# First queries in pieces, batch 1's keys first, base 3 summed with bases 0 to 2, and batch 1's copies on other queues

## The chip, the core and the metric

The kernel runs on one core of a Trainium2 chip. A core has five engines with an instruction queue each: TensorE (PE, matrix products into PSUM), VectorE (DVE), ScalarE (ACT), GpSimd (POOL) and SyncE (SP, which here only issues DMAs). ACT and POOL can issue DMAs too, in their own queues. An engine takes its queue in order, so an instruction that waits holds up everything behind it on that engine. The metric is the device time of one execution in microseconds (us), as the median of several runs.

## What is computed

Eight sequences of 256 tokens of width 512 pass through a gated attention block and a gated feed forward:

```python
x = x + tanh(g_xattn) * attention(layernorm(x), ctx)      # 32 heads of 16, 8 key heads
x = x + tanh(g_ffn) * feed_forward(layernorm(x))

# attention
q = heads(concat([ctx, h]) @ Wq)                          # Wq 1024 x 512
k, v = heads(h @ Wk), heads(h @ Wv)
ssm_k, ssm_v = heads(ctx @ Wsk), heads(ctx @ Wsv)
scores = q @ [ssm_k, k].T / sqrt(16) + alibi              # each query sees 64 keys back, in both halves
o = softmax(scores) @ [ssm_v, v];  return o @ Wo

# feed forward
probs = softmax(xt @ w_router);  topk of 4 among 128 experts
gate, up = xt @ w_gate, xt @ w_up                         # 8 bases of 256 columns
basis = silu(gate) * up
mixed = weighted sum of the 8 bases, weights from the experts' squared amplitudes
return mixed @ w_down + silu(xt @ sg) * (xt @ su) @ sd    # sg, su: two more pieces of 256 columns
```

## The kernel before

**Batches and stages.** A batch is one sequence: two tiles of 128 tokens. For each of the eight batches there are four stages: `project` (norm, transposes, keys, queries, values), `attention`, two `tail`s (one for each tile: output projection, second norm, transposes, router) and `feed_forward`. They are generators that issue a few instructions and yield a weight; `run` takes the one with the smallest time first, so that the work of one batch's attention and the next but one batch's projection is laid between the products of a batch's feed forward. `start(gen, length, at, total)` sets the pace of a generator. The order on every engine's queue is fixed in this way when the program is built; on the chip nothing is reordered.

**The start.** Loads stand first (lines 112 to 145): the context `ctT` of batch 0 and the first half of its `x` on SP; `wsk`, the first half of `wq`, `wk`, the second half of `x`, the second half of `wq`, `wsv`, `wv` and batch 1's `x` and context on ACT, ahead of ACT's table load (`warm`). PE runs 14 transposes of the identity (`idle`, line 171). `project_first` then makes the first tile's keys (`pk`, line 389) and queries (`pq`, line 402), group by group in four banks, and transposes `x`. `rest` makes batch 0's values and the second tile's keys and queries between the steps of its attention, and goes on with `project(1)`. The bank that it takes alternates between the tag `one` and `gu2`.

**Attention.** `score` makes the products of queries and keys (line 628), `soften` adds the bias and takes the smallest value (DVE, line 641), `exponentials` runs on ACT (660), `divide` on POOL (672), `turn` transposes blocks on DVE (685), `values` multiplies by the values (PE, 707). The values lie in `vbd`, copied by DMA from `vpad` (`diagonals`, line 496) in 16 copies for each batch: SP and POOL issue them for batch 0, SP alone for the others. `first_batch` is batch 0's form.

**Feed forward.** There are ten pieces `k` of 256 columns: eight bases, two shared pieces. Each is a product of two by two blocks, done as seven block products (Winograd's form) instead of eight; it needs sums of weight blocks. The tokens' sums `sT` are made for each batch, the weights' sums once: `sub` subtracts two blocks (line 953), `keep` stores the result in device memory (957), and later batches load it (`load_gu`: 7 loads of 256 KB for a summed piece, 4 for one that isn't). A piece's loads are issued two pieces ahead, when the block that used the buffer is done (`after`). For bases 2, 0 and 1, in this order, `first_weights` sums during batch 0's attention, all on POOL; for pieces 3 to 9 the first feed forward does it, in the piece ahead (`more`, `late`), the first two subtractions on DVE and the other two on POOL. `wgu` holds two pieces at a time.

The block products of a piece go to two PSUM banks: `m15` and then `m76`, then 2 and 3 into the first, 4 into the second. ACT copies `u`, `m5` and `m7` out and computes the tanh `th`; a bank is free when the values in it have been used. There are three such banks.

**Steps of the tail.** `po` (line 866) is the output projection, `tr_f` the transposes of the second norm's result, `pl` the router's product, `pst` and `pc` turn the selection into coefficients, with ACT's copy `selT` between the two.

The names in the profile leave numbers out: `sc<-kT,qT` is a score product, `sc<-pt,vbd` a values product, `m<-w,hT` and `m<-w,sT` block products.

Of the kernel before, what the change touches and what calls it, by code (L numbers as in the profile page):

```python
# [15 lines left out]
P = 128  # L16
# [16 lines left out]
MASKED = 1e32  # L33
WARM = 14


@with_exitstack
def gated_block(
# [93 lines left out]

    def load_queries(half):
        nc.scalar.dma_start(
            wq_sb[:, half * NC : (half + 1) * NC, :],
            wq[half * HID : (half + 1) * HID].rearrange("(c p) n -> p c n", p=P),
        )

    load_queries(0)
    wk_sb = weight(wk, HID, HK * D, "wk", nc.scalar)  # L140
    nc.scalar.dma_start(x_0[:, 1, :], x[0, P:, :])
    load_queries(1)
    wsv_sb = weight(wsv, HID, HK * D, "wsv", nc.scalar)
    wv_sb = weight(wv, HID, HK * D, "wv", nc.scalar)
    loaded[1] = load(1, nc.scalar), load_context(1, nc.scalar)

# [20 lines left out]
    warm = const.tile([P, 1], F32, tag="warm", name="warm")  # L167
    nc.scalar.activation(warm, neghalf[:, :1], AF.Tanh)
    idle = next_bank("idle")
    for _ in range(WARM):  # L170
        nc.tensor.transpose(idle[:, 0, :P], ident, ident)

# [96 lines left out]
    def first_weights():  # L269

        for k in (2, 0, 1):
            for g in range(1, 5):
                load_gu(k, g)
            if k == 2:
                yield 2.0
                later["wd"] = weight(w_down, I, HID, "wd", nc.sync)


                later["sd"] = sd = const.tile([P, NSI // 2, HID], F32, tag="sd", name="sd")
                nc.sync.dma_start(  # L280
                    sd, sw_down.rearrange("(j o p) n -> o p j n", o=2, p=P)[1]
                )
            if k == 0:
                yield 5.5
                yield from first_sums(2)
        yield 1.0
        yield from first_sums(0)
        yield 1.0
        yield from first_sums(1)
# [84 lines left out]
    def project_first():  # L374
# [25 lines left out]
        def queries(pq, g, cols, cs):  # L400
            for c in cs:
# [4 lines left out]
                )  # L406

        def put_queries(pq, g, t):
            blocks = slice(t * NB // NT, (t + 1) * NB // NT)
# [8 lines left out]
        keys(pk, 0, slice(0, T))  # L418
        evict = transposed(xnT, first_normed[0], 0, "x0", lambda shape, name: early(name, NC))
        pqs = [next_bank(f"pq_0_{g}")[:, 0, :P] for g in range(G - 1)]  # L420
        pqs.append(ps_one.tile([P, P], F32, tag="one", name="pq_0_3"))
        for g in range(G):
            queries(pqs[g], g, tiles[0], range(NC))
        put_keys(pk, 0, slice(0, T))
        evict()
        evict = transposed(xnT, first_normed[1], 1, "x0", lambda shape, name: early(name, NC))
        keys(pk, 1, tiles[0])
        for g in range(G):
            queries(pqs[g], g, tiles[0], range(NC, 2 * NC))
        put_keys(pk, 1, tiles[0])  # L430
# [76 lines left out]
    def project(b, xns=None):  # L507
# [18 lines left out]
        xnT = two.tile([P, NC, T], F32, tag="xo", name=f"xnT_{b}")  # L526
        if b == 1:
            yield BEFORE
        for t in range(NT):
            yield from own()  # L530
            evict = transposed(xnT, xns[t], t, f"x{b}", bank)
            yield AFTER if b == 1 else AFTER - 0.8
            evict()
            free()
            yield BEFORE if b == 1 else BEFORE + 0.8


        kT = two.tile([P, 2, 2, T], F32, tag="kT", name=f"kT_{b}")
        yield from own()
        pk = bank([P, 2, T], f"pk_{b}")  # L540
        for s, (w_sb, src) in enumerate(((wsk_sb, ctT), (wk_sb, xnT))):
            for c in range(NC):
# [3 lines left out]
                )  # L546
            yield AFTER if s else MORE
        for par in range(2):
# [4 lines left out]
        free()  # L553
        yield BEFORE


# [22 lines left out]
        for t in range(NT):  # L579
            for s, (w_sb, src) in enumerate(((wsv_sb, ctT), (wv_sb, xnT))):  # L580
                for c in range(NC):
# [10 lines left out]
    def attention(b):  # L592
# [185 lines left out]
        for u in range(2 * n + 4):  # L778
# [193 lines left out]
    def feed_forward(b):  # L972
# [324 lines left out]
```

## Time and profile before

| | us |
|---|---|
| median of 3 runs | 1021.93 |
| lowest and highest | 1018.09, 1021.96 |
| the profiled execution, its own time | 1023.29 |
| span of its trace | 1021.4 |
| DVE waits for the chain of PE's last output projection of batch 0 (L866) | 8.41 |
| POOL busy from 60 to 80 us, from 80 to 100 us | 14.86, 5.61 |
| PE busy from 100 to 150 us | 43.23 |
| PE busy from 150 to 200 us | 50.00 |

In the profile's windows every row is a stretch of time from the span's start, with the busy time of each engine in it; PE's granted clock is 1.00 at full speed. In the timeline a row gives the start, the duration, the engine and line, the operation, its output and inputs, the count, and in brackets how long the engine had been idle before it and who released it. `ACTq`, `SPq` and `POOL ... DMA_DIRECT2D` rows are issues of DMAs. An fp32 matrix product shows as two records.

### The profile page before, as it was taken

How to read it: one execution, taken by the hardware profiler on the slowest of the kernel's cores; microseconds unless marked ns; L12 is line 12 of the kernel's file. 1: busy time of each engine (PE TensorE's matmuls, PEld its weight loads, DVE VectorE, ACT ScalarE, POOL GpSimd, SP SyncE). 2: the span in 40 equal slices, each digit the busy share in tenths (PEclk: the TensorE clock that was granted, in tenths of full speed). 3: DMA queues.
4: the chain of work that ended last, by engine and by line, in shares of the span. 5: the costliest groups of instructions: out<-in, count | busy, mean ns of one | idle time of the engine just before them, and what ended most of it. 6: DMA issues, size and time to landing. Idle time of an engine off the chain costs nothing.

```text
span 1021.4 us, 27843 instructions
## 1 busy us (share of the span) xinstructions
PE 989.7 (97%) x10470; PEld 799.9 (78%) x10470; DVE 601.0 (59%) x2241; ACT 442.0 (43%) x1657; POOL 470.2 (46%) x892
## 2 busy tenths in 40 slices
PE   8888799899999999999999999999999999999998
PEld 8666687777888687886778868788787977787886
DVE  2764766757564675636855378544665466765453
ACT  3652454335542455415543255433554335442231
POOL 4773576734553255523644236342455225661341
PEclk9999999999999999999999999999999999999999
DMA  6942845569545694447844577455964468665891
GB/s 206 231 145 79 252 146 151 170 199 288 175 137 154 180 301 142 152 141 217 282 141 146 163 214 256 125 166 165 267 204 140 133 191 257 203 195 174 271 302 66
DMA packets 117302, 192.15 MB, mean 188 GB/s; under 512 B 12848, under 2 KB 34864, under 8 KB 117168
## 3 DMA queue, kind: packets, MB, share of 16 engines
q1 hardware_dynamic: 112672, 184.87, 58.9%
q10 hardware_dynamic: 4112, 4.46, 1.3%
q8 instruction: 83, 1.36, 0.5%
q0 software_dynamic: 384, 1.05, 0.5%
q14 instruction: 51, 0.42, 0.1%
HBM read 158.87 MB, written 14.68 MB: 170 GB/s over the span
## 4 chain that ended last, share of the span: by engine, by line
PE 87%; DVE 5%; issue 2%; POOL 2%; ACT 2%; DMA 1%; SPq 0%; ACTq 0%; DVEq 0%; POOLq 0%
PE m L1001 38%; PE m L1010 10%; PE pq L562 8%; PE sc L707 6%; PE po L866 5%; PE sc L628 5%; PE pd L1144 4%; PE pk L543 2%; PE pv L582 2%; PE pd L1147 2%; POOL pr L672 1%; PE pq L402 1%; PE pl L896 1%; DVE pr L641 1%; ACT pr L660 1%
## 5 line engine op out<-in xcount | busy, mean ns | idle before, releaser
L672 POOL TENSOR_SCALAR pr<-pr,rd 128x192 f32<-128x192 f32 (+2 forms) x512 | 210.9, 430 | 251.6 <-DVE rd L669 234.3
L660 ACT ACTIVATE pr<-pr,nm 128x192 f32<-128x192 f32 (+2 forms) x512 | 218.9, 430 | 110.0 <-DVE nm L641 58.7
L1001 PE MATMUL m<-w,sT 128*128 128x256 f32 x1024 | 253.1, 381 | 1.1 <-DMA w<-in_L_ffn_w_up 0.7
L1001 PEld LDWEIGHTS m<-w,sT 128*128 128x128 f32 x1024 | 194.5, 191 | 29.0 <-issue 1.2
L641 DVE CUSTOM_DVE_ANT_1 pr<-sc,nbias 128x192 f32<-128x192 f32 (+2 forms) x512 | 154.0, 322 | 99.8 <-PE sc L628 92.9
L1001 PE MATMUL m<-w,hT 128*128 128x256 f32 x768 | 204.9, 390 | 1.0 <-DVE u L1046 1.0
L1001 PEld LDWEIGHTS m<-w,hT 128*128 128x128 f32 x768 | 140.1, 191 | 25.6 <-issue 6.3
L1091 POOL TENSOR_TENSOR mixed<-mixed,th 128x256 f32<-128x256 f32 x112 | 81.2, 725 | 137.8 <-DVE th L1086 137.8
L685 DVE STREAM_TRANSPOSE pt<-pr 128x768 f32<-128x768 f32 (+2 forms) x128 | 111.5, 871 | 4.6 <-POOL pr L672 3.0
L660 ACT ACTIVATION_READ_ACCUMULATOR pr<-pr,nm 128x1 f32 x512 | 97.9, 191 | 0.0
L1047 POOL TENSOR_TENSOR m<-m,u 128x256 f32<-128x256 f32 x80 | 61.2, 765 | 67.8 <-DVE u L1046 58.9
L963 ACT ACTIVATE th<-m 128x256 f32<-128x256 f32 x80 | 30.8, 384 | 138.2 <-DVE up L1057 138.1
L707 PEld LDWEIGHTS sc<-pt,vbd 64*32 64x32 f32 x5120 | 61.1, 106 | 26.3 <-issue 14.2
L707 PE MATMUL sc<-pt,vbd 64*32 64x64 f32 (+2 forms) x5120 | 69.0, 229 | 9.1 <-DVE nm L641 5.2
L1069 DVE TENSOR_TENSOR gate<-u,m 128x256 f32<-128x256 f32 x80 | 33.3, 416 | 72.4 <-PE m L1001 66.9
L1057 DVE TENSOR_TENSOR up<-u,m 128x256 f32<-128x256 f32 x80 | 33.3, 417 | 67.6 <-PE m L1001 40.7
L628 PE MATMUL sc<-kT,qT 32*128 32x192 f32 (+2 forms) x1024 | 64.9, 336 | 4.6 <-DVE nm L641 4.1
L628 PEld LDWEIGHTS sc<-kT,qT 32*128 32x128 f32 x1024 | 45.1, 184 | 28.3 <-DVE nm L641 9.4
L963 ACT ACTIVATE th<-gate 128x256 f32<-128x256 f32 x80 | 33.2, 416 | 76.7 <-DVE gate L1069 76.7
L1010 PE MATMUL m<-sT,w 128*128 128x128 f32 x512 | 66.1, 278 | 0.0
L1010 PEld LDWEIGHTS m<-sT,w 128*128 128x128 f32 x512 | 62.3, 194 | 0.4
L1144 PE MATMUL pd<-sd,shT 128*128 128x512 f32 x128 | 61.5, 603 | 0.2 <-DVE shT L1080 0.2
(131 smaller groups left out, 1375.7 us busy)
## 6 DMA issues: line engine op xcount, KB each, us to landing
w<-s SPq DMA_DIRECT2D x284, 256.0 KB, 3.5
w<-in_L_ffn_w_gate SPq DMA_DIRECT2D x130, 256.0 KB, 3.1
w<-in_L_ffn_w_up SPq DMA_DIRECT2D x73, 256.0 KB, 4.0
vbd<-vpad SPq DMA_DIRECT2D x120, 128.0 KB, 3.2
s<-w SPq DMA_DIRECT2D x40, 256.0 KB, 3.4
w<-in_L_ffn_shared_w_gate SPq DMA_DIRECT2D x32, 256.0 KB, 2.7
w<-in_L_ffn_shared_w_up SPq DMA_DIRECT2D x18, 256.0 KB, 3.7
sd<-in_L_ffn_shared_w_down SPq DMA_DIRECT2D x16, 256.0 KB, 3.4
```

The costliest lines, as they stand in the source:

```text
L562: nc.tensor.matmul(pq, lhsT=wq_sb[:, c, g * P : (g + 1) * P], rhs=(ctT if c < NC else xnT)[:, c % NC, :], start=(c == 0), stop=(c == 2 * N ...
L628: nc.tensor.matmul(seen(scs[p][:, j * COLS : (j + 1) * COLS], qb), lhsT=qT[rows, qb].rearrange("p g q -> p (g q)"), rhs=kT[rows, par, :, f ...
L641: nc.vector.tensor_tensor_reduce(out=part, in0=seen(scs[p][:, j * COLS : (j + 1) * COLS], qb0 + j), in1=bass.AP(tensor=bias.tensor, offset ...
L660: nc.scalar.activation(part, part, AF.Exp, bias=nmax, scale=-1.0, accum_out=den)
L672: nc.gpsimd.tensor_scalar(part, part, rden[:, p : p + 1], 1.0, op0=ALU.mult, op1=ALU.mult)
L685: nc.vector.transpose(pt[:, u % 4].rearrange("p c (s k) -> p (c s) k", s=2)[:, :, lo:], pr.rearrange("p c (s k) -> p (c s) k", s=2)[:, :, ...
L707: nc.tensor.matmul(scs[gp][32 * c : 32 * (c + 1), 2 * COLS + lo * Q : 2 * COLS + hi * Q], lhsT=vbd[rows, kb % (P // Q), kb // (P // Q) * 2 ...
L963: nc.scalar.activation(th, gate, AF.Tanh, scale=0.5)
L1001: nc.tensor.matmul(dst, lhsT=sides_of[m][c], rhs=w[:, c, :], start=(first and c == 0), stop=(c == NC // 2 - 1), skip_group_check=True,)
L1010: nc.tensor.matmul(dst[:, cols], lhsT=w[:, c, cols], rhs=sides_of[m][c], start=(first and ic == c == 0), stop=(c == NC // 2 - 1), skip_gro ...
L1091: nc.gpsimd.tensor_add(mixed[t], mixed[t], th)
L1144: nc.tensor.matmul(po, lhsT=shT[:, ic, t * P : (t + 1) * P], rhs=down[ic], **flags)
```

## The change

First, the queries' weights come in eight loads of 256 KB instead of two of 1 MB. ACT's table load stands behind the first four; `wk`, the second half of `x` and the other four follow. `wsv`, `wv` and batch 1's input are issued by ACT only after the first eviction of `xnT`. The first tile's queries run chunk by chunk over all four groups, three chunks ahead of the transposes of `x` and one behind. The 14 transposes of the identity become 9 matrix products.

Second, in batch 1's projection the context's keys come ahead of the transposes of `x`, which use the bank `gu2`; the input's keys follow. `rest` starts its alternation with the other bank.

Third, `first_weights` sums base 3 too: the order is 2, 3, 0, 1, and its pace changes. The first feed forward sums and stores pieces 4 to 9.

Fourth, the copies to `vbd` of batch 1 are issued by ACT (two groups) and POOL (two groups) instead of SP, and batch 2's `x` and context are loaded by ACT instead of SP.

```diff
-WARM = 14
+WARM = 9
...
-    load_queries(0)
-    wk_sb = weight(wk, HID, HK * D, "wk", nc.scalar)
-    nc.scalar.dma_start(x_0[:, 1, :], x[0, P:, :])
-    load_queries(1)
-    wsv_sb = weight(wsv, HID, HK * D, "wsv", nc.scalar)
-    wv_sb = weight(wv, HID, HK * D, "wv", nc.scalar)
-    loaded[1] = load(1, nc.scalar), load_context(1, nc.scalar)
+    def load_queries(cs):
+        for c in cs:
+            nc.scalar.dma_start(wq_sb[:, c, :], wq[c * P : (c + 1) * P, :])
+
+    load_queries(range(NC))
...
     nc.scalar.activation(warm, neghalf[:, :1], AF.Tanh)
+    wk_sb = weight(wk, HID, HK * D, "wk", nc.scalar)
+    nc.scalar.dma_start(x_0[:, 1, :], x[0, P:, :])
+    load_queries(range(NC, 2 * NC))
     idle = next_bank("idle")
     for _ in range(WARM):
-        nc.tensor.transpose(idle[:, 0, :P], ident, ident)
+        nc.tensor.matmul(idle[:, 0, :P], lhsT=ident, rhs=ident, start=True, stop=True)
...
-        for k in (2, 0, 1):
+        for k in (2, 3, 0, 1):
             for g in range(1, 5):
                 load_gu(k, g)
...
-            if k == 0:
+            if k == 3:
                 yield 5.5
                 yield from first_sums(2)
+                yield 1.0
+                yield from first_sums(3)
...
+        def first_queries(pqs, cs):
+
+            for c in cs:
+                for g in range(G):
+                    queries(pqs[g], g, tiles[0], [c])
...
-        evict = transposed(xnT, first_normed[0], 0, "x0", lambda shape, name: early(name, NC))
...
-        for g in range(G):
-            queries(pqs[g], g, tiles[0], range(NC))
+        first_queries(pqs, range(NC - 1))
+        evict = transposed(xnT, first_normed[0], 0, "x0", lambda shape, name: early(name, NC))
+        first_queries(pqs, [NC - 1])
         put_keys(pk, 0, slice(0, T))
         evict()
+        wsv_sb = weight(wsv, HID, HK * D, "wsv", nc.scalar)
+        wv_sb = weight(wv, HID, HK * D, "wv", nc.scalar)
+        loaded[1] = load(1, nc.scalar), load_context(1, nc.scalar)
+        later.update(wsv=wsv_sb, wv=wv_sb)
         evict = transposed(xnT, first_normed[1], 1, "x0", lambda shape, name: early(name, NC))
         keys(pk, 1, tiles[0])
-        for g in range(G):
-            queries(pqs[g], g, tiles[0], range(NC, 2 * NC))
+        first_queries(pqs, range(NC, 2 * NC))
...
-                if banks[0] % 2:
+                if banks[0] % 2 == 0:
                     return other_bank(2, name)
...
-    def diagonals(qd, eng):
+    def diagonals(qd, *engs):
...
-            eng.dma_start(
+            engs[g * len(engs) // G].dma_start(
...
-            loaded[b] = load(b), load_context(b)
+            eng = nc.scalar if b == 2 else nc.sync
+            loaded[b] = load(b, eng), load_context(b, eng)
...
+        if b == 1:
+
+            yield BEFORE
+            yield from own()
+            pk = bank([P, 2, T], f"pk_{b}")
+            keys(pk, 0)
+            for t in range(NT):
+                yield MORE
+                evict = transposed(
+                    xnT, xns[t], t, f"x{b}",
+                    lambda shape, name: other_bank(2, name).rearrange("p (c n) -> p c n", n=P),
+                )
+                yield AFTER
+                evict()
+            yield BEFORE
+            keys(pk, 1)
+            yield AFTER
...
-                    diagonals(2 * (u - 1) + step, nc.sync)
+
+                    diagonals(2 * (u - 1) + step, *((nc.scalar, nc.gpsimd) if b == 1 else (nc.sync,)))
...
-            late = b == 0 and k > 2
-            more = b == 0 and 2 < k + 1 < PIECES
+            late = b == 0 and k > 3
+            more = b == 0 and 3 < k + 1 < PIECES
...
-    start(first_weights(), 0.39, at=-0.537, total=20.5)
+    start(first_weights(), 0.40, at=-0.537, total=25.5)
```

More of the change, by code (lines that the diff above doesn't have):

```diff
@@ L131, in gated_block @@
     wq_sb = const.tile([P, 2 * NC, HID], F32, tag="wq", name="wq")
[L133 to L137, printed above, removed]
-    load_queries(0)
-    wk_sb = weight(wk, HID, HK * D, "wk", nc.scalar)
-    nc.scalar.dma_start(x_0[:, 1, :], x[0, P:, :])
-    load_queries(1)
-    wsv_sb = weight(wsv, HID, HK * D, "wsv", nc.scalar)
-    wv_sb = weight(wv, HID, HK * D, "wv", nc.scalar)
-    loaded[1] = load(1, nc.scalar), load_context(1, nc.scalar)
+    def load_queries(cs):
+        for c in cs:
+            nc.scalar.dma_start(wq_sb[:, c, :], wq[c * P : (c + 1) * P, :])
+    load_queries(range(NC))
     ident = const.tile([P, P], F32, tag="ident", name="ident")
@@ L526, in project, with keys @@
         xnT = two.tile([P, NC, T], F32, tag="xo", name=f"xnT_{b}")
[L527 to L535, printed above, removed]
         kT = two.tile([P, 2, 2, T], F32, tag="kT", name=f"kT_{b}")
-        yield from own()
-        pk = bank([P, 2, T], f"pk_{b}")
-        for s, (w_sb, src) in enumerate(((wsk_sb, ctT), (wk_sb, xnT))):
+        def keys(pk, s):
+            w_sb, src = ((wsk_sb, ctT), (wk_sb, xnT))[s]
             for c in range(NC):
@@ L546, in project @@
                 )
-            yield AFTER if s else MORE
+        if b == 1:
[14 more added lines that the diff above has]
+            yield AFTER
+        else:
+            for t in range(NT):
+                yield from own()
+                evict = transposed(xnT, xns[t], t, f"x{b}", bank)
+                yield AFTER - 0.8
+                evict()
+                free()
+                yield BEFORE + 0.8
+            yield from own()
+            pk = bank([P, 2, T], f"pk_{b}")
+            for s in range(2):
+                keys(pk, s)
+                yield AFTER
         for par in range(2):
@@ L554, in project @@
         yield BEFORE
+        if b == 1:
+            yield BEFORE
         qT = two.tile([P, NB, G, Q], F32, tag="qT", name=f"qT_{b}")
@@ L579, in project @@
         for t in range(NT):
-            for s, (w_sb, src) in enumerate(((wsv_sb, ctT), (wv_sb, xnT))):
+            for s, (w_sb, src) in enumerate(((later["wsv"], ctT), (later["wv"], xnT))):
                 for c in range(NC):
```

## The prediction

> **What bounds the kernel now.** I read the busy shares first, then the windows by stage, then the timelines and waits of the stages that are not full. TensorE (PE) is busy 97% of the span. From 300 us on there is nothing to win: 298.64 of 300 us busy between 300 and 600. What this change touches lies before 130 us, and PE is not full there.
>
> ```profile
> PE 989.7 (97%) x10470; PEld 799.9 (78%) x10470; DVE 601.0 (59%) x2241; ACT 442.0 (43%) x1657; POOL 470.2 (46%) x892
> ```
> The windows (columns: stage and its length, busy time and instructions of PE, weight load, VectorE (DVE), ScalarE (ACT), GpSimd (POOL), then PE's granted clock, DMA share, GB/s):
>
> ```profile
> 40.00:60.00 20.00, 15.70 (x214) 11.63 (x214) 11.76 (x53) 13.20 (x54) 13.09 (x24) 0.96 0.83 251
> ...
> 95.00:100.00 5.00, 4.48 (x17) 3.89 (x18) 4.06 (x22) 2.43 (x11) 1.48 (x6) 0.66 0.58 144
> ...
> 120.00:125.00 5.00, 1.11 (x4) 0.65 (x4) 3.58 (x11) 0.48 (x2) 1.10 (x2) 0.85 0.85 315
> 125.00:130.00 5.00, 3.65 (x69) 3.13 (x70) 4.92 (x17) 2.27 (x10) 4.84 (x5) 0.50 0.02 6
> ```
> There are three soft places: the start, 42 to 97 us, and 120 to 130 us, where the clock is also halved after the idle time. As PE is full later, a microsecond won here should reach the end whole.
>
> **Part A, the start.** The timeline of PE:
>
> ```profile
> 1.37 3.25 PE L171 MATMUL idle<-ident 128*128 128x128 f32 x14 [1.37 <-POOL neghalf L150]
> ...
> 5.68 3.78 PE L389 MATMUL pk<-ctT,wsk 128*128 128x256 f32 x8 [1.07 <-DMA wsk<-in_L_xattn_Wsk]
> ...
> 10.11 4.09 PE L402 MATMUL pq<-ctT,wq 128*128 128x128 f32 x32
> ```
> Later, eight records of this keys product (L543) take 1.99 us. Here they take 3.78: PE is at half speed in spite of 14 transposes (the profile's clock column doesn't show it this early). The change makes the warm-up nine matmuls, two records each like every fp32 product here: 18 x 0.236 (half the 0.47 per 256 columns) = 4.25 us, from 1.37 to 5.6. By the row alone: full speed came with the queries, at about 10.5, 4.8 us after the first real matmul; from 1.37 that gives 6.2, and the keys end at about 7.9 instead of 9.47: 1.6 saved. The Trainium skill ("TensorE: Matmul & The Clock Gate", Parts 1 and 4) says that transposes don't count as activity, and that a free-running window of about 3.4 us must be busy. By it the clock rises between 4.8 and 8.2: 1.9 to 0.6 saved. Here the row's 1.6 stands.
>
> First queries: now all 1 MB of a half must land (1.26 + 9.0 = 10.26). In four pieces, and with wk and x's second half behind the table load, ctT, wsk, x's first half and the four pieces are 2.1 MB; the DMA rate of the first 20 us (about 1.1 MB by 5.5 us, then 380 GB/s) brings them by 8.3, so the pieces don't hold PE after the keys: three pieces 24 x 0.111 = 2.7 -> 10.6, transposes 0.44, fourth 0.9 -> 11.9. Next is late: x's second half, 2.6 MB in, lands at 9.8, its norm takes the 2.3 of now (10.63 to 12.96) -> 12.1; transposes, keys, 32 records: 0.44 + 0.89 + 3.56 -> 17.0. All four groups now end together, so four evictions of 0.29 end at 17.6, against 19.43. **A = 1.8 us** (0.6 to 2.2). wsv, wv and batch 1's input, issued at 11.3 behind the eviction, hold ACT for about 2 us (four issues of 0.5); behind them stand the second keys copy and xnT's second half, wanted only by 17; wsv lands by 14.5, wanted at 18. The table load now stands ahead of wk's issue: 1.28 us, with the pieces still in flight.
>
> **Part B, 20 to 97 us.** What goes: with batch 1's context keys first and transposes in another bank, PE's waits for ACT at 45.01 (0.70), 47.24 (1.58) and 55.18 (1.66, kT), three of four waits of 0.47 for qT, and, since po of the second half now has pq_3, pv and sc_0 behind it, 1.29 + 0.68 at 94 to 96 with their slow clock (1.5). Sum 8.8.
>
> What comes: base 3's four subtractions, 4 x 1.27 on POOL (L953; 16 instead of 12 before the first feed forward), and, as bases 2 and 3 fill the two buffers, base 0's loads only behind the last store of base 3. POOL now:
>
> ```profile
> 43.98 1.62 POOL L672 TENSOR_SCALAR pr<-pr,rd 128x192 f32<-128x192 f32 x4 [4.39 <-DVE rd L669]
> 46.22 1.62 POOL L672 TENSOR_SCALAR pr<-pr,rd 128x192 f32<-128x192 f32 x4 [0.61 <-DVE rd L669]
> 47.81 1.28 POOL L953 TENSOR_TENSOR w<-w,w 128x512 f32<-128x512 f32 x1
> ...
> 77.03 1.62 POOL L672 TENSOR_SCALAR pr<-pr,rd 128x192 f32<-128x192 f32 x4
> 78.59 0.10 POOL L905 MEMSET prob<- 128x4 f32 x1
> 78.66 2.63 POOL L953 TENSOR_TENSOR w<-w,w 128x512 f32<-128x512 f32 x2
> 92.07 0.55 POOL L184 TENSOR_TENSOR rs_f<-ve_f,neghalf 128x1 f32<-128x1 f32 x1 [10.78 <-DVE ve_f L182]
> ```
> In the changed order (times in the old clock, without A) POOL runs full from 44: last subtraction of base 3 done at 65.6, base 0's loads (SP's next in line) issued 66 to 67.7, landed 70.5; behind the first subtraction that waits for them POOL has the last two divides: subtraction, pr_14, two subtractions, pr_15: 70.5 + 1.3 + 1.6 + 2.6 + 1.6 = 77.6, against 78.65. With one transpose on DVE the last values product starts at 78.6 instead of 80.07, though PE would be there at about 73: most of the 8.8 turns into this wait. From there PE has 1.9 + 1.73 (pq_3's first half, which stood ahead of it) + po 3.43 + 1.73 + 0.67 + 1.78 + 0.76 + 0.44 + 1.78 + 0.9 = 15.1, so the feed forward starts at 93.7, not 96.8, and warm (0.9 more): 4.0. If PE cools in the 5 us wait, it loses up to 1.7 again. **B = 3.5 us** (1 to 8).
>
> **Part C, first feed forward.** PE now, by its timeline:
>
> ```profile
> 95.52 1.50 PE L896 MATMUL pl<-wr,hT 128*128 128x128 f32 x8 [0.68 <-ACT hT L205]
> ...
> 119.98 1.13 PE L1001 MATMUL m<-w,sT 128*128 128x256 f32 x4 [0.73 <-DMA w<-in_L_ffn_w_up]
> 126.35 1.55 PE L707 MATMUL sc<-pt,vbd 64*32 64x96 f32 x64 [5.24 <-DVE nm L641]
> ```
> and what DVE does meanwhile:
>
> ```profile
> 121.31 0.69 DVE L953 TENSOR_TENSOR w<-w,w 128x512 f32<-128x512 f32 x1 [3.50 <-DMA w<-in_L_ffn_w_up]
> ```
> DVE's first subtraction of base 3 waits 3.5 us for a load that SP issued at 114.78, behind the copies to vbd and batch 2's input, and that took 6.5 us to land (median 4.0). Everything on DVE behind it waits, so the values product waits 5.24. With base 3 summed before, this goes: 0.73 + 5.24 + about 2.0 at half clock = 8.0. The next candidate is base 4: its loads come one piece later, 3.5 to 5 us landing against some 6.5 us until it is wanted: no wait. Base 3's seven loads instead of four (0.75 MB more) are made good by its four stores that leave this stage.
>
> What comes: eight of sixteen vbd copies and x_2, ctT_2 stand in ACT's in-order queue, between the exponentials and PSUM copies that free PE's banks. The built program takes eight completion counters in turn for the copies of SP and ACT together, and each copy waits for the transfer that had its counter before; so the seventh vbd copy waits until x_2 has landed. On SP four such issues take 2.53 to 3.11 us, 0.65 each. Queued behind on ACT: selT (then pc on PE), th of piece 0 (then the bank of piece 1's m76), u and m5 of piece 1 (then its m23). From the feed forward's start: issues done 1.3 to 5.5, selT 6.8 (PE ready 6.3: 0.5); x_2 7.6, th 10.5, bank free 10.9 (PE ready 9.5: 1.4); x_2 landed 12.5 (+4.4 and a little, by the row of SP's x loads), two issues, four exponentials of 0.44, copies: 15.9 (PE ready 12.7: 3.2). Sum 5.1. If x_2 lands as slowly as on ACT's row at the start (8.9 us), 9.3. I take 6.5, nearer to the first, as the DMA share here (0.85 to 0.93) has SP's rows in it. POOL's eight issues of 0.57 fall into its gaps.
>
> Here a rule speaks against the change: "DMA: Bandwidth & Descriptors", Issuing engines are not separate DMA queues: all issuers share sixteen engines, spreading saves only issue time. The row agrees in what leaves SP (11.0 us of issue), but that was no wait of PE's by itself: by the rule the copies' move wins nothing and costs the 6.5; only by the row of the load stuck behind SP's copies would it have saved about 2 of the 3.5, which the early sum saves already. **C = 8.0 - 6.5 = 1.5 us** (-4 to 7).
>
> The other edits (bank parity, the values weights through a dictionary, pacing of later batches by equal numbers) change neither work nor waits.
>
> **Sum.** 1.8 + 3.5 + 1.5 = 6.8. The profiled execution took 1023.29 (span 1021.4): 1016.5 there. It is 1.4 above the median of the runs; from 1021.93 the forecast is **1015.1 us**.
>
> **Rivals.** (1) ACT's issues hide: its 43% share and its idle 1.44 us at 100.12 speak for it, the order of its queue against. 1.8 + 3.5 + 8.0 = 13.3: 1008.6. (2) Waits only move: PE cools at both new waits and x_2 lands slowly: 1.8 + 2.3 + 8.0 - 9.3 - 1.7 = 1.1: 1020.8. For it: each idle spell above was followed by a halved clock. (3) Slower: **ACT's queue** becomes the bound of the first feed forward. Its ten issues add ten times their excess over 0.65 to a chain on which PE already waits. The gain is gone when an issue costs 1.3, and at 1.9, the mean of its three slow issues at 3.66 to 9.4 (2.11, 1.71, 1.85), it is 6.8 - 12.5 = 5.7 lost: 1027.6. SP's vbd copies beside POOL's took 1.26 (10.11 for 8) with the DMA full; that this came in one burst speaks against.
>
> **Chances.** Forecast 0.42, rival 1 0.20, rival 2 0.26, rival 3 0.12. About 0.5% (5 us) is what can be told from no change: faster 0.62, same 0.26, slower 0.12. Forecast's own range 1011 to 1017; 1006 to 1023 takes in rivals 1 and 2.
>
> **What would show it.** A: keys records near 2 us and first scores at 17.6. B: an idle PE ahead of the last values product (73 to 78), released by POOL's divide; feed forward at 92. C: no DVE wait on L953's successor near 120; PE waits behind ACT's u, th, selT in the ten us after the feed forward's start. I am wrong if ACT's issues cost nothing, if base 4's subtraction waits for its loads instead, or if later batches are no longer full.

## The result, and the profile after

| | kernel before | changed kernel | ratio, 95% interval |
|---|---|---|---|
| first comparison, 6 runs each | 1019.17 | 1027.32 (1022.53 to 1031.26) | 1.0066 (1.0046 to 1.0086) |
| second comparison, 22 runs of the changed kernel | 1021.21 | 1022.85 (1018.85 to 1028.80) | 1.0019 (1.0008 to 1.0030) |
| third comparison, 22 runs of the changed kernel | 1020.89 | 1022.89 (1019.17 to 1025.93) | 1.0018 (1.0007 to 1.0028) |

The change makes the kernel slower, by 0.2 to 0.7%: the sign is the same in three comparisons, the size is not. The size goes with the granted clock: its mean over the runs was 0.985 in the first comparison, 0.990 and 0.989 in the other two; why it was lower in the first is not shown. The forecast was 1015.1, so its sign was wrong. The profiled execution of the changed kernel took 1025.07, its span 1023.3.

The page's busy times say nothing of it: PE is at 97% as before.

```profile
PE 991.4 (97%) x10474; PEld 802.0 (78%) x10474; DVE 598.8 (59%) x2239; ACT 441.4 (43%) x1657; POOL 474.5 (46%) x902
```

The windows of the changed kernel (columns as in the prediction) show where it lies:

```profile
40.00:60.00 20.00, 17.03 (x208) 12.76 (x206) 9.21 (x44) 12.00 (x50) 12.96 (x22) 0.76 0.77 239
...
95.00:100.00 5.00, 5.00 (x52) 4.75 (x51) 2.78 (x15) 2.39 (x9) 3.08 (x5) 1.00 0.28 105
...
105.00:110.00 5.00, 3.48 (x19) 2.71 (x12) 1.97 (x9) 2.08 (x10) 2.85 (x6) 0.76 1.06 285
110.00:115.00 5.00, 2.59 (x9) 1.89 (x8) 1.65 (x8) 0.38 (x1) 2.12 (x6) 0.84 1.06 300
115.00:120.00 5.00, 3.83 (x13) 2.55 (x12) 2.26 (x11) 4.10 (x17) 1.79 (x4) 0.72 1.08 304
120.00:125.00 5.00, 5.00 (x37) 4.21 (x36) 4.77 (x24) 3.73 (x17) 4.03 (x8) 1.00 1.08 268
125.00:130.00 5.00, 5.00 (x96) 4.09 (x95) 4.90 (x18) 1.75 (x9) 3.15 (x8) 1.00 0.66 223
```

The hole that stood at 120 to 130 us (PE busy 1.11 and 3.65 of 5) is gone, and one of the same kind stands at 105 to 120, with the clock below 1. From 40 to 60 us PE is busier than before because it runs at a lower clock (0.76 instead of 0.96), not because it does more.

PE's timeline, by the steps that the prediction had named:

```profile
5.89 1.99 PE L386 MATMUL pk<-ctT,wsk 128*128 128x256 f32 x8 [0.44 <-DMA wsk<-in_L_xattn_Wsk]
...
13.22 0.66 PE L199 MATMUL tr_x<-ident,xn_a 128*128 128x128 f32 x4 [1.32 <-DVE xn_a L185]
...
18.71 0.73 PE L657 MATMUL sc<-kT,qT 32*128 32x64 f32 x16 [0.37 <-ACT qT L413]
...
51.54 2.04 PE L736 MATMUL sc<-pt,vbd 64*32 64x96 f32 x112 [1.48 <-DVE pt L714]
53.51 3.40 PE L539 MATMUL pk<-xnT,wk 128*128 128x256 f32 x8
...
81.21 0.73 PE L736 MATMUL sc<-pt,vbd 64*32 64x32 f32 x48
83.60 1.67 PE L736 MATMUL sc<-pt,vbd 64*32 64x96 f32 x144 [1.67 <-DVE rrd L941]
...
98.86 1.03 PE L1031 MATMUL m<-w,hT 128*128 128x256 f32 x4
```

and in the kernel before the feed forward's first product:

```profile
96.81 1.91 PE L1001 MATMUL m<-w,hT 128*128 128x256 f32 x4
```

The warm-up works: the first keys take 1.99 instead of 3.78 us. Then PE waits 1.32 us for the second half of `x` to land and be normalized, and the first scores start at 18.71 (before 19.47, forecast 17.6). At 51.54 a values product waits 1.48 us for a transposed block, and the keys behind it take 3.40 us where eight records at full clock take 1.99. PE reaches the last values product at 81.21 and, after the first 48 of its records, waits 1.67 us, until 83.60. The feed forward starts at 98.86: before it was 96.81, the forecast was 92.

What POOL does ahead of these two waits:

```profile
46.23 2.63 POOL L983 TENSOR_TENSOR w<-w,w 128x512 f32<-128x512 f32 x2
...
75.59 1.27 POOL L983 TENSOR_TENSOR w<-w,w 128x512 f32<-128x512 f32 x1 [3.37 <-DMA w<-in_L_ffn_w_up]
```

Two subtractions in a row stand ahead of the divide (at 48.84) that PE's 51.54 needs; in the kernel before none stands there, as the divide at 46.22 follows that at 43.98 directly. And a subtraction of base 0 waits 3.37 us for its load, with the last divides behind it.

In the first feed forward ACT's timeline (`ACTq` is an issue of a DMA by ACT) and PE's list of waits (us in total, times, longest) belong together:

```profile
104.70 0.61 ACTq L502 DMA_DIRECT2D vbd<-vpad  x1
105.36 0.40 ACT L689 ACTIVATE pr<-pr,nm 128x128 f32<-128x128 f32 x1 [3.60 <-DMA w<-in_L_ffn_w_gate]
...
115.85 0.45 ACT L689 ACTIVATE pr<-pr,nm 128x192 f32<-128x192 f32 x1 [2.56 <-DMA w<-in_L_ffn_w_gate]
```

```profile
PE m L1031 <- DVE th L998: 2.4, 1, 2.4
...
PE pc L968 <- ACT selT L963: 1.5, 1, 1.5
...
PE m L1031 <- ACT m L1064: 1.2, 1, 1.2
```

The exponential at 105.36 needs no weights. What waited for the load of a gate block was the copy to `vbd` ahead of it, which stood at 101.9 to 104.7 until that load had freed its completion counter. PE's three waits are those that the prediction worked out (0.5, 1.4 and 3.2: 5.1 by its own sum; 1.5, 2.4 and 1.2 here: 5.1).

### The profile page after: what moved, and what is told of

Read it like the earlier page. It is cut to its first block, busy times and chain, and to the rows that moved or that the text cites. A ratio compares the mean times of both kernels' runs of the same rounds, so it can differ in the third digit from the quotient of the medians.

```text
span 1023.3 us, 27856 instructions
## 1 busy us (share of the span) xinstructions
PE 991.4 (97%) x10474; PEld 802.0 (78%) x10474; DVE 598.8 (59%) x2239; ACT 441.4 (43%) x1657; POOL 474.5 (46%) x902
## 4 chain that ended last, share of the span: by engine, by line
PE 84%; DVE 6%; DMA 3%; ACT 2%; POOL 2%; issue 1%; SPq 1%; ACTq 0%; DVEq 0%; POOLq 0%
PE m L1031 37%; PE m L1040 9%; PE pq L591 9%; PE sc L736 6%; PE po L896 5%; PE sc L657 5%; PE pd L1174 4%; PE pv L611 3%; PE pk L539 2%; PE pd L1177 2%; DMA w<-in_L_ffn_w_gate 1%; ACT pr L689 1%; POOL w L983 1%; POOL pr L701 1%; SPq L502 1%
## 5 line engine op out<-in xcount | busy, mean ns | idle before, releaser
L701 POOL TENSOR_SCALAR pr<-pr,rd 128x192 f32<-128x192 f32 (+2 forms) x512 | 208.8, 427 | 228.2 <-DVE rd L698 204.4
L1031 PE MATMUL m<-w,sT 128*128 128x256 f32 x1024 | 254.0, 382 | 2.4 <-DVE th L998 2.4
L736 PE MATMUL sc<-pt,vbd 64*32 64x96 f32 (+2 forms) x5120 | 71.7, 234 | 7.4 <-DVE pt L714 3.6
L657 PEld LDWEIGHTS sc<-kT,qT 32*128 32x128 f32 x1024 | 45.2, 184 | 29.1 <-DVE nm L670 10.5
```

The lines of the kernel that those rows point to most:

```text
L657: nc.tensor.matmul(seen(scs[p][:, j * COLS : (j + 1) * COLS], qb), lhsT=qT[rows, qb].rearrange("p g q -> p (g q)"), rhs=kT[rows, par, :, f ...
L701: nc.gpsimd.tensor_scalar(part, part, rden[:, p : p + 1], 1.0, op0=ALU.mult, op1=ALU.mult)
L736: nc.tensor.matmul(scs[gp][32 * c : 32 * (c + 1), 2 * COLS + lo * Q : 2 * COLS + hi * Q], lhsT=vbd[rows, kb % (P // Q), kb // (P // Q) * 2 ...
L1031: nc.tensor.matmul(dst, lhsT=sides_of[m][c], rhs=w[:, c, :], start=(first and c == 0), stop=(c == NC // 2 - 1), skip_group_check=True,)
```

## The experiments

Three marks in PE's timeline cut the path: K, the first record of batch 1's context keys; F, the first block product of batch 0's feed forward; E, the last product of the shared down projection of batch 1 (`pd<-sd`). From E to the span's end all traces take 663.5 to 665.4 us, so E stands for the end. Every kernel was compared with the kernel before on its own chip. From `start_only` on the table stands in groups of four, and the runs of one group ran on one chip. A single trace is one execution: between those of one kernel F moves by up to 3.5 us and E by up to 7, so the ratios decide on a time, and the marks on a place where several traces agree.

| run | what it has | K | F | F - K | E | E - F | ratio, 95% interval |
|---|---|---|---|---|---|---|---|
| before | | | 96.8 | | 357.2 | 260.4 | |
| changed | | 42.9 | 98.9 | 56.0 | 359.1 | 260.2 | 1.0066 (1.0046 to 1.0086) |
| start_only | start | | 96.9 | | 356.5 | 259.6 | 1.0002 (0.9990 to 1.0014) |
| start_keys | start, keys first | 40.8 | 91.5 | 50.7 | 355.4 | 263.9 | 0.9986 (0.9975 to 0.9997) |
| sp_all | changed, copies on SP | 42.3 | 97.9 | 55.5 | 361.3 | 263.4 | 1.0016 (1.0005 to 1.0027) |
| late3 | changed, base 3 late | 40.8 | 91.5 | 50.7 | 352.6 | 261.1 | 0.9963 (0.9948 to 0.9977) |
| after2 | changed | 42.6 | 99.2 | 56.5 | 361.6 | 262.4 | 1.0019 (1.0008 to 1.0030) |
| after_x2e | changed, input 2 early | 41.9 | 96.9 | 55.0 | 357.5 | 260.6 | 1.0013 (1.0001 to 1.0025) |
| late3_x2e | base 3 late, input 2 early | 42.8 | 93.6 | 50.8 | 351.9 | 258.3 | 0.9985 (0.9972 to 0.9999) |
| late3_pool_x2e | the same, copies on POOL | 42.8 | 94.7 | 51.8 | 352.5 | 257.8 | 0.9956 (0.9941 to 0.9970) |
| late3b | late3 again | 41.4 | 92.7 | 51.3 | 353.0 | 260.3 | 0.9980 (0.9968 to 0.9991) |
| late3_pool | base 3 late, copies and input 2 on POOL | 41.9 | 92.7 | 50.8 | 354.3 | 261.6 | 1.0000 (0.9987 to 1.0013) |
| after_pool | changed, copies and input 2 on POOL | 42.2 | 98.9 | 56.7 | 358.6 | 259.7 | 1.0055 (1.0035 to 1.0076) |
| pool_twice | start_keys, four more subtractions | 41.1 | 95.1 | 54.0 | 356.3 | 261.2 | 1.0015 (1.0003 to 1.0027) |
| after_c | changed | 40.9 | 96.0 | 55.2 | 356.6 | 260.6 | 1.0018 (1.0007 to 1.0028) |
| sp_all_c | sp_all again | 39.5 | 94.4 | 54.9 | 354.0 | 259.6 | 1.0006 (0.9995 to 1.0018) |
| after_pool_x2e | changed, copies on POOL, input 2 early | 42.6 | 99.3 | 56.7 | 353.3 | 254.0 | 0.9959 (0.9946 to 0.9972) |
| best_c | late3_pool_x2e again | 40.9 | 91.8 | 50.9 | 349.4 | 257.7 | 0.9937 (0.9917 to 0.9956) |

"Copies" are batch 1's sixteen to `vbd`, "input 2" is batch 2's `x` and context, 1 MB.

### The start alone

The kernel before with the diff's first part and nothing else.

> Kernel before with the start of the changed kernel alone (nine warm-up matmuls, first queries in four pieces, values weights and batch 1's input loaded later). The prediction's term for the start: 1.8 us gained whole, first scores at 17.6. What the changed kernel's trace suggests: 0.8 us gained, first scores at 18.7, PE's idle 1.3 us ahead of the second normalized half. Rival: the 0.8 us is lost again before 100 us because later loads come later (batch 1's input): no change, feed forward at 96.8 as before.

The first scores start at 18.73 (0.74 earlier), yet F is where it was, and the time is the same. PE's timeline of this run shows where the gain went:

```profile
43.70 0.66 PE L199 MATMUL tr_x<-ident,xn_a 128*128 128x128 f32 x4 [0.70 <-ACT xnT L200]
45.94 3.28 PE L548 MATMUL pk<-ctT,wsk 128*128 128x256 f32 x8 [1.58 <-ACT xnT L200]
49.15 1.28 PE L633 MATMUL sc<-kT,qT 32*128 32x192 f32 x16
```

and the same place in the kernel before:

```profile
47.24 1.99 PE L543 MATMUL pk<-ctT,wsk 128*128 128x256 f32 x8 [1.58 <-ACT xnT L205]
49.16 0.93 PE L628 MATMUL sc<-kT,qT 32*128 32x192 f32 x16
```

The new start is 1.3 us ahead there. The waits of 0.70 and 1.58 us are the same in both, but here the clock is halved behind them (0.62 and 0.53 in the windows of 46 to 50 us; 1.00 before), which costs 1.29 + 0.35 = 1.6 us. The gain is eaten at once. The rival was right that it is lost before 100 us, but not by the later loads that it named.

### Keys first, with base 3 late and all copies on SP

```diff
-        for k in (2, 3, 0, 1):
+        for k in (2, 0, 1):
...
-                    diagonals(2 * (u - 1) + step, *((nc.scalar, nc.gpsimd) if b == 1 else (nc.sync,)))
+                    diagonals(2 * (u - 1) + step, nc.sync)
```

(the rest of the diff's third and fourth parts is undone in the same way)

> The start, and batch 1's context keys first with the other bank order; base 3 summed late and all copies on SyncE as before. If the prediction's list of removed waits holds (8.8 us between 42 and 97 us) and only base 3's subtractions on GpSimd spoilt it, the feed forward starts at about 89 to 91 us instead of 96.8, and the time is 5 to 7 us below the kernel before. If keys first only moves the waits to the values' diagonals and to the divide, the feed forward starts at 95 to 97 and the time is within 2 us of it.

F is 91.5, 5.4 us earlier: the first theory's place. But the time is only 0.14% lower. PE's timeline has a new wait, and its list of waits has another in the feed forward:

```profile
62.68 1.43 PE L655 MATMUL sc<-kT,qT 32*128 32x192 f32 x12 [2.73 <-DVE nm L668]
```

```profile
PE m L1029 <- DMA w<-in_L_ffn_w_up: 7.3, 1, 7.3
```

Of the 8.8 us of waits that the prediction removed, 2.73 came back as a wait of scores for the smallest value: PE is there before DVE has freed the bank. And the feed forward, started 5.4 us earlier, waits 7.3 us for weights. Keys first has changed SP's order as well: the kernel before issues all sixteen copies (94.29 to 111.56) and then batch 2's input (111.60); here the input goes first, at 102.11, and the last eight copies stand behind it, one of them waiting 2.1 us until the context has landed. The weights come behind these.

### The copies back on SP, base 3 early

```diff
-            eng = nc.scalar if b == 2 else nc.sync
+            eng = nc.sync
...
-                    diagonals(2 * (u - 1) + step, *((nc.scalar, nc.gpsimd) if b == 1 else (nc.sync,)))
+                    diagonals(2 * (u - 1) + step, nc.sync)
```

> The changed kernel with batch 1's copies and batch 2's input back on SyncE: the start, keys first and the early base 3 stay. Theory that ScalarE's queue costs the first feed forward some 8 us: 6 to 9 us below the changed kernel, about 1019 to 1021, no PE wait behind tanh, u or m at 106 to 120 us. Rival that the early base 3 (GpSimd's subtractions, late loads of base 0) is what costs: no more than 2 us below the changed kernel, feed forward still at 98 to 99 us, and SyncE's loads late, so that a wait on a base's load takes the place of ScalarE's.

The ratio is 1.0016: below the changed kernel's first comparison (1.0066), no different from its later two (1.0019 and 1.0018), so the rival's side. F is still at 97.9, and in the chain of waits (start, us, what) a weight load stands near the place where base 3's stood:

```profile
110.92 9.57 DMA vbd<-vpad
120.48 0.02 issue
120.50 7.00 DMA w<-in_L_ffn_w_up
127.50 0.04 issue
127.54 2.08 PE m L1031 x4
```

SP's list of waits from 105 to 122 us has in it:

```profile
SPq L502 <- DMA x<-in_x: 1.8, 1, 1.8
SPq L502 <- DMA ctT<-in_ctx: 1.7, 1, 1.7
```

SP issued `x` of batch 2 at 108.35 and its context at 108.83, then four copies and two weight loads. The next copy is the eighth issue after `x`, the one behind it the eighth after the context: each waits until the transfer whose counter it takes has landed. So these four copies take from 115.9 to 120.2; only then is the load for base 2's last block issued, and it lands 7 us later. PE waits 10.9 us (8.9 in `sp_all_c`). In this kernel base 3 is already summed, so the early sum does not keep the stage free of such a stall. It is not quite the stall of the kernel before: there SP was held only 0.7 us for the context, and the load, issued at 114.78 behind the copies and the input, took 6.5 us to land.

### Base 3 late, the copies left on ACT and POOL

```diff
-        for k in (2, 3, 0, 1):
+        for k in (2, 0, 1):
...
-            late = b == 0 and k > 3
-            more = b == 0 and 3 < k + 1 < PIECES
+            late = b == 0 and k > 2
+            more = b == 0 and 2 < k + 1 < PIECES
```

> The changed kernel with base 3 summed in the first feed forward again, as in the kernel before; start, keys first and the queues of ScalarE and GpSimd stay. Theory that GpSimd's four more subtractions and the late loads of base 0 cost: feed forward at 93 to 95 us instead of 98.9, and the stall near 120 us, with the copies off SyncE, 2 us instead of 8: 4 to 8 us below the changed kernel. Theory that ScalarE's queue costs: the queue waits stay, the stall on base 3's load comes on top of them: no gain on the changed kernel, or slower.

0.9963, and 0.9980 when it was run again:

> Base 3 summed late with ScalarE's and GpSimd's copies again, on the chip of the runs beside it: 0.996 to 0.998 of the kernel before, feed forward at 91.5 us.

(`first_weights` has its old pace too.) F is 91.5 and 92.7. This one undo turns the loss (1.0066, 1.0019 and 1.0018, in other groups) into a gain. Its list of waits from 90 to 150 us still has ACT's queue in it, and a shorter wait (`nm`, 2.3 us) at the kind of product where the old stall stood (5.24):

```profile
PE m L1029 <- DVE th L996: 3.2, 1, 3.2
PE sc L734 <- DVE nm L668: 2.3, 1, 2.3
PE pc L966 <- ACT selT L961: 0.9, 1, 0.9
```

So both sides of the expectation came true in their own stage: the early base 3 costs ahead of F, ACT's queue costs behind it. The stall near 120 us stays away without the early sum: 2.3 us are left of it, where the changed kernel has 1.6, and E - F is 261.1 and 260.3 against 260.2 to 262.4 in the changed kernel. With the copies and the input where the change puts them, the traces show no gain of the early sum in this stage.

### GpSimd's load by itself

In `start_keys`, base 2's subtractions on POOL are repeated, four more of 1.27 us; results and SP's order stay.

```diff
-        sub(k, 1, nc.gpsimd)
+        more = 1 if k == 2 else 0
+        for _ in range(1 + 2 * more):
+            sub(k, 1, nc.gpsimd)
...
-        sub(k, 2)
+        for _ in range(1 + more):
+            sub(k, 2)
...
-        sub(k, 4)
+        for _ in range(1 + more):
+            sub(k, 4)
```

> Start and keys first with base 3 late and all copies on SyncE (0.9986 of the kernel before, feed forward at 91.5 us), with base 2's subtractions on GpSimd repeated so that four more of 1.27 us stand between its divides at 46 to 56 us; SyncE's order of loads is untouched. Theory that GpSimd's load is what the early base 3 costs ahead of the feed forward: feed forward at 94 to 97 us. Rival that the late loads of base 0 behind eight stores cost it: feed forward no later than 92.5 us.

F is 95.1. F - K rises from 50.7 to 54.0, and the time by 0.3%, as much as the early base 3 costs in `sp_all`. One wait carries it (from 34 to 150 us, longest 5.5, where `start_keys` has 2.7):

```profile
PE sc L659 <- DVE nm L672: 7.2, 2, 5.5
```

Over all runs F - K is 50.7 to 51.8 in the seven traces with base 3 late (mean 51.0, `pool_twice` aside), and 54.9 to 56.7 in the eight with base 3 early (mean 55.8): 4.8 us. `pool_twice` shows that GpSimd's load alone can cost 3.3, but at another place: its four subtractions hold up the scores at `nm`, and the first output projection comes 10.5 us after K as in `start_keys`. With base 3 early this projection comes 13.5 us after K in the mean, with base 3 late 11.0. So some 2.5 of the 4.8 us are lost by there, with the wait for `pt` (0.9 to 1.7 us) and the slow keys behind it; the other 2.3 come up to the second output projection, with the wait behind base 0's late loads (in the lists under DVE's `rrd`, 1.3 to 3.2 us in every trace with base 3 early, in none without). The late loads were not changed by themselves.

In the time it is mostly less. In four pairs on one chip each, the early base 3 costs 2.4 us (`sp_all` and `start_keys`), 2.4 (`after_x2e` and `late3_x2e`), 4.8 (`after_pool` and `late3_pool`) and 1.2 (`after_pool_x2e` and `best_c`, whose intervals overlap).

### Which queue, and what stands in it

First, batch 2's input out of the stage, loaded by SP between base 0's and base 1's sums:

```diff
         yield from first_sums(0)
+        loaded[2] = load(2), load_context(2)
         yield 1.0
```

> The changed kernel with batch 2's input loaded by SyncE between base 0's and base 1's subtractions (about 88 us, where the DMA engines are nearly idle) instead of by ScalarE inside the first feed forward. Theory that ScalarE's queue waits for the landing of batch 2's input and for DMA engines that are full from 100 to 126 us: 3 to 5 us below the changed kernel, PE's wait behind tanh shorter. Rival that only the early base 3 costs: no more than 1 us, feed forward still at 98 to 99 us.

> Base 3 summed late, copies by ScalarE and GpSimd (the version that took 0.9963 of the kernel before), and batch 2's input loaded by SyncE after base 0's sums, about 75 us. Theory that the first feed forward is bound by the transfers of 95 to 115 us (DMA share 1.02 to 1.15): 1 MB less there at about 300 GB/s is 3.5 us, so 0.993 of the kernel before. Rival that the wait is the order of ScalarE's queue and the counters it shares with SyncE: the wait behind tanh (3.2 us) stays, 0.996.

> The changed kernel again, unchanged, for a second trace and a comparison on the same chip as the runs beside it. Theory of the two opposed parts (the early base 3 costs 6 to 7 us ahead of the first feed forward; ScalarE's queue takes the blocked copies out of SyncE's way and pays some of it back): ratio to the kernel before between 1.002 and 1.007, feed forward at 98 to 99 us. Rival, that the early base 3 with ScalarE's queue is worse by itself than with SyncE's (1.0016): ratio at 1.006 or more.

Nothing is gained: 1.0013 beside 1.0019 for the changed kernel on the same chip (at the low end of what was expected of it), and 0.9985 with base 3 late, where 0.993 or 0.996 was expected. So 1 MB less for the DMA engines is by itself not what the stage lacks, although their share is above 1.0 there. ACT is still held behind its copies, 3.70 us for the landing of one of SP's gate loads and 4.22 for that of an earlier copy; PE's wait only moves from `th` (4.2 to 0.7 us) to the copy of `m5` (1.1 to 4.1).

Second, all copies and the input to GpSimd, whose copies have eight counters of their own in the built program:

```diff
-            eng = nc.scalar if b == 2 else nc.sync
+            eng = nc.gpsimd if b == 2 else nc.sync
...
-                    diagonals(2 * (u - 1) + step, *((nc.scalar, nc.gpsimd) if b == 1 else (nc.sync,)))
+                    diagonals(2 * (u - 1) + step, nc.gpsimd if b == 1 else nc.sync)
```

> The changed kernel (base 3 early) with all of batch 1's copies and batch 2's input on GpSimd instead of half on ScalarE: the price of ScalarE's queue by itself, 6.5 us by the prediction. Theory that ScalarE's queue costs: 3 to 6 us below the changed kernel, no wait of PE behind tanh, selT or the copy of m5; feed forward still at 98 to 99 us. Rival that in this stage something else ends next (GpSimd's divides behind its issues, the weight loads): less than 1.5 us.

> Base 3 summed late, all of batch 1's copies and batch 2's input issued by GpSimd, none by ScalarE. Theory that ScalarE's in-order queue is the cost of the move (PE's waits behind tanh and selT, 4.1 us with the slow clock behind them): 2 to 4 us below the run beside it with ScalarE's copies, 0.993 to 0.995 of the kernel before. Rival that the DMA engines (full at 95 to 112 us) set the stage: no gain, PE waits for GpSimd's divide or a weight load instead.

Neither theory nor rival foresaw the first result: 1.0055, as slow as the changed kernel's first comparison (1.0066) and slower than the other two (1.0019, 1.0018). With base 3 late it is 1.0000 beside 0.9980. The timeline of `after_pool` shows the queue stuck in the same way, now behind the landing of the context (issued at 107.11, eight issues before the copy that waits for it until 118.96), with the divide behind it:

```profile
118.96 0.55 POOL L502 DMA_DIRECT2D vbd<-vpad  x1 [2.65 <-DMA ctT<-in_ctx]
119.55 1.63 POOL L701 TENSOR_SCALAR pr<-pr,rd 128x192 f32<-128x192 f32 x4
...
121.21 0.98 DVE L714 STREAM_TRANSPOSE pt<-pr 128x768 f32<-128x768 f32 x1 [6.06 <-POOL pr L701]
```

Third, both together:

> As the run beside it (base 3 late, batch 2's input at about 75 us), with all sixteen of batch 1's copies issued by GpSimd and none by ScalarE. Theory that ScalarE's in-order queue is what PE waits for behind tanh and the copies of u and m5: these waits go, 1 to 3 us below the run beside it. Rival that the DMA engines bound the stage, or that GpSimd's issues (0.57 us each, eight more) now delay its divides: no gain, the wait moves to the divide.

> The changed kernel (base 3 early) with all of batch 1's copies on GpSimd and batch 2's input loaded by SyncE at about 88 us. Theory that what costs is standing in any in-order queue behind the landing of batch 2's input: neither ScalarE nor GpSimd stands behind it now, 3 us or more below the changed kernel, feed forward still at 97 to 99 us. Rival that the stage is set by the DMA engines' full load: within 1.5 us of the changed kernel.

> Base 3 late, batch 1's copies on GpSimd, batch 2's input early: 0.9956 of the kernel before on the earlier chip; 0.994 to 0.997 here, below the kernel before and below the changed kernel by 5 us or more.

Now it pays: with base 3 early 0.9959, 5.9 thousandths below the changed kernel on the same chip, although F is at 99.3; E - F falls to 254.0. Its waits from 34 to 150 us:

```profile
PE m L1033 <- DVE th L1000: 1.6, 1, 1.6
...
PE m L1033 <- DMA w<-in_L_ffn_w_up: 1.1, 1, 1.1
```

With base 3 late the same arrangement took 0.9956 and 0.9937 (1015.49 beside 1020.89), the fastest version of this study, and faster than both kernels. Moving the input or the copies alone gained nothing, both together did. What was not run is the input early with all copies left on SP; how much of the gain needs GpSimd stays open.

Last, the move of the copies beside an early base 3, on one chip:

> The changed kernel, on the chip of the runs beside it. If the move of the copies pays beside the early base 3: 2 to 4 us below the version with all copies on SyncE. If it does nothing: within 1.5 us of it. If ScalarE's queue costs what the prediction priced (6.5 us, less what SyncE gains): 3 us or more above it.

> The changed kernel with batch 1's copies and batch 2's input on SyncE, on the same chip: 1.0016 of the kernel before again, PE's wait of about 10 us on a base's load near 117 to 127 us.

1.0018 with ACT, 1.0006 with SP, 1.0 us apart in the medians: the intervals overlap, and the move as the change makes it neither pays nor costs more than 1 or 2 us here. Beside a late base 3 it may gain a little (0.9963 in the group of `start_keys` and 0.9980 in another, 0.9986 without the move; the intervals of the last two overlap).

## Why the prediction was wrong, by its steps

The step that failed is part B's: that PE reaches the last values product at about 73 and that the early base 3 costs only a wait there. In the means of the changed kernel's three traces F is at 98.0, 1.2 us behind the kernel before, where A and B had it 5.3 ahead: a miss of 6.5 us. Behind F the miss is 2.2: E - F is 261.1 against 260.4, where C had it 1.5 shorter.

**A, 1.8 us: about 0.** The warm-up, the keys and the four pieces came as written: the first keys end at 7.88, as the row's 1.6 us said (7.9; by the rule that transposes don't count as activity it was 1.9 to 0.6, which agrees). The second half of `x` was later than in the sum (its transposes start at 13.22, forecast 12.1), so 0.75 us were left at the first scores; and the halved clock at 46 us took them in `start_only`.

**B, 3.5 us: the other sign, the failed step.** The list of waits, 8.8 us, gave 5.4 in F (`start_keys` against the kernel before) and 4.2 in the mean of the seven traces with base 3 late: the term left out is the wait of 2.73 us for DVE's `nm`, which PE meets when it comes earlier. In `start_keys` PE starts the last values product at 75.78, before it was 80.07; forecast was about 73. In the changed kernel's three traces PE reaches it at 78.4 to 81.2. The place on GpSimd's queue was found rightly: base 3's last subtraction ends at 68.69 (forecast 65.6), base 0's first starts at 75.59 (70.5), and PE waits for the divides behind it. But this wait is 1.6 to 2.9 us and not 5, as PE has lost its time before: POOL's subtractions already hold a divide at 46 to 49, PE waits 1.5 us at 51.5, and the keys behind run at a lower clock (2.6 to 3.8 us instead of 1.99 in all eight traces with base 3 early, in one of the seven with base 3 late). The prediction put this place at nothing. It named cooling, for the later wait only ("If PE cools in the 5 us wait, it loses up to 1.7 again"), and took 0.5 off for it (4.0 to 3.5). The products behind the last values product took 15.3 us, as forecast (15.1).

**C, 8.0 - 6.5 = 1.5 us: about right in size, credited to the wrong edit.** The old stall went, as written: 5.24 us before, 1.6 in the changed kernel. The waits behind ACT's queue came, 5.1 us as worked out. But "With base 3 summed before, this goes" gives the 8.0 to the early sum. With base 3 late and the copies off SP only 2.3 us of the stall are left, and E - F is the same (`late3`, `late3b`); in single traces with all copies on GpSimd it is 1.9 and 3.7 us shorter with base 3 early, so a part of the 8.0 may be the early sum's there. With base 3 early and the copies on SP, PE waits 8.9 and 10.9 us for the next load (`sp_all_c`, `sp_all`). The prediction dismissed that next load with "no wait". And what it priced as ACT's queue did not go with ACT alone (`after_pool`, 259.7), nor when batch 2's input alone left the stage (`after_x2e`, 260.6); only with both is the stage shorter (`after_pool_x2e`, 254.0 in one trace, 6 us in the time), with base 3 late by 3. The rule of the Trainium skill that was weighed ("DMA: Bandwidth & Descriptors", Issuing engines are not separate DMA queues) says that another issuer saves only issue time; the runs agree as far as the transfers go (the DMA share from 105 to 120 us is 1.05 to 1.08 in the changed kernel and in `after_pool_x2e`), and show what it leaves out here: a copy that waits for its counter holds up the engine that issues it (3.60 us of ACT, 2.65 of POOL), and what that engine was doing decides the price.

**The rivals.** Rival 3, ACT's queue as the bound, gave 1027.6, and the first comparison 1027.32. That is no confirmation: its waits are in the trace, but without ACT's queue and with SP's (`sp_all_c`) the time is still not below the kernel before. The loss is base 3's, ahead of F; ACT's queue only failed to earn it back. Rival 2 ("waits only move") had the mechanism that most of the runs show, at 1020.8. Its argument that "each idle spell above was followed by a halved clock" does not hold, though: in the kernel before the keys behind the wait of 1.58 us at 47.24, and the queries behind that of 1.66 at 55.18, took 1.99 us, their time at full clock.

## What to carry to other kernels

Before a stall is put down to the load that it names, look at what stood ahead of that load in its issuer's queue: a kernel that takes the load away can meet a stall at the next one. Keep long transfers from standing among short copies that take their counters in turn, and put the copies on an engine where little waits behind them; half of such a move can be worth nothing or less, as each half was here. And work put on a lightly loaded engine "for free" must be checked against the short operations that the busiest engine waits for, at each place and not at the end alone.

## What the runs showed of the hardware

The clock falls after idle spells shorter than expected, and not always after the same ones: 0.70 and 1.58 us of waiting within 3 us left the clock at 1.00 in the kernel before and halved it for some 4 us in `start_only`, where the same waits came 1.3 us earlier. The Trainium skill ("TensorE: Matmul & The Clock Gate", Part 1) says that the window in which activity is counted runs freely, which fits a price that depends on the moment; it gives about 3.4 us of idleness for the fall, and here it fell after 1.58. Four transposes stand between the two waits; if they don't count as activity, as the prediction had it, the spell is 2.9 us in both kernels, still less than 3.4.

This may also make part of the scatter. At 37 to 38 us a values product waited 0.2 to 0.9 us for its copies to `vbd` in 9 of the 16 traces with keys first, and K came at 41.4 to 42.9 (mean 42.4) in these, at 39.5 to 41.9 (mean 40.8) in the other 7. With a wait of half a microsecond goes a delay of 1.6; from 40 to 42 us the clock was 0.50 to 0.90 in the nine, and 1.00 in six of the seven. That the wait is the cause is not shown: the clock was already low from 36 to 40 us in nearly all of them. Whether a run has it differs from execution to execution of one kernel (`after2` and `after_c`).
